# Attended values loaded with the sums, other due times, and queries and keys in a buffer of their own, in a fused attention and mixture-of-experts layer

## The chip, the cores and the metric

One core of a Trainium2 chip. The kernel is one launch. Its time is the device time in microseconds (us) of that core. The core has TensorE (PE; its weight loads are shown apart as PEld), VectorE (DVE), ScalarE (ACT), GpSimd (POOL) and SyncE (SP), each of which works through its own instructions in their order, and 16 DMA engines that the queues of SP, ACT and POOL feed.

## The reference

The input `x` has 4 sequences of 1024 tokens with 256 channels. Two blocks follow each other.

```python
x = x + attn(_layernorm(x), w_attn, w_proj)       # 16 heads of 16, causal, ALiBi bias
x = x + ffn(_layernorm(x), ...)

# ffn, with T, B, C = x.shape: the second attention runs over the 4 sequences, at each token place
qkv = x @ in_proj_w.T + in_proj_b
scores = einsum('tbhd,sbhd->bhts', q, k) * scale   # t, s: the 4 sequences
ctx = einsum('bhts,sbhd->tbhd', softmax(scores), v)
h = _layernorm(x + ctx @ out_w.T + out_b) * ln1_g + ln1_b
probs = softmax(h @ router_w.T + router_b)
assign = max(top_k(probs, 2)[1])                   # one of 8 experts for each token
out = gelu(h @ w1[e].T + b1[e]) @ w2[e].T + b2[e]  # e = assign
return _layernorm(h + out) * ln2_g + ln2_b
```

## The kernel before

Two versions of the layer are in the program: `fast_layer`, which always runs, and `general_layer`, which runs only where a check of the sums asks for it, and did not here. Everything below is `fast_layer`.

**Attention.** The 1024 tokens of a sequence are cut in 4 chunks of 256. A batch is one chunk of one sequence; there are 16, the sequence changing fastest. A unit is what is attended at a time: a whole batch in the first three chunks (units 0 to 11), one block of 128 tokens in the last chunk (units 12 to 19: the first block of the four sequences, then the second). For each unit and each group g of 4 heads, in rounds of 512 columns, `score` makes products of keys and queries (`sk<-slots`), ACT takes the exponential (`p<-sk`), POOL zeroes what is not causal (L1005), and `weigh` makes products with the values (`pv<-p,v`). Keys and queries of the next unit are loaded into the `slots` buffers by SP (L958), as soon as the scores of the current one have been issued; the loads go by way of a copy in DRAM (`k`), which is written from `kq`, a copy that DVE makes of TensorE's projection.

**The end of a unit.** Values carry a column of ones, so each head's sum of exponentials comes out of the same product. The result `yt` is stored to DRAM (`y`, L1057). Then, each at a due time: `load_sums` (L1064) loads the sums, a row per head, from `y`; `invert` (L1071) has DVE take the reciprocal and stores it to DRAM (`r`); `load_y` (L1079) loads the reciprocals, spread over the channels (`su`, L1090), and the attended values, turned (`yc`, L1093); `divide` (L1096) multiplies them on DVE; `project` (L1105) multiplies with `wp` on TensorE and adds to `x` (`x<-x,op`). Unit 19, the last, goes another way: `normalise` makes its sums with a product and inverts them on DVE, `project_slots` projects.

**Fronts.** A front (`front`, L1573) is the second attention and the choice of expert for one block of 128 token places of all four sequences; there are 8 (0 to 7). It is a generator; each `yield` names the kind of the next piece (`E`, `P`: DVE; `D`, `d`: products; `N`: ACT; `R`: a square root on POOL) and its cost. Its pieces: norm statistics; `u` (normalised); `utF`, transposes of `u` to `ut`; the projection into `qkv` (queries, keys, values and router columns together); four scores on DVE (`pr`, `sc`); softmax; four weighted sums on DVE (`pv`, `ctx`); transposes; the output projection `ao`; a norm; the choice (`key` to `hot`); counting and ranks (`place`). The buffer `qkv` exists once: a front may begin the projection (`DQ`) only when `held["qkv"]` is free, which it becomes after the weighted sums (L1720). Front 7 (`last`) puts norms and copies on ACT.

**Experts.** After front 5 a first table of tiles of 128 tokens is made (`tabulate_first`: `count`, `own`, `in_tile`, `who_first`, `rows`, `at_w`), after front 7 a second (`tabulate_rest`: `who`). A tile is gathered by POOL (`given`, L1839), turned (`mtp`), goes through the two weights (`hid`, `oe`), is normed by DVE and scattered to `out` by POOL (L1955). 18 tiles belong to the first table, 20 to the second. The first four tiles load their own weights (L1857); all weights are loaded after attention (L2310). All this lies after attention.

**The order.** The order on each engine is written by a planner in the program while it is built. It keeps an imagined clock of PE, DVE and ACT. In the main loop (L2273) two rounds of scores and one of weighing form a step, with an `E_slot` (L2219) after each scoring, in which due DVE work and transfers are emitted, and one `D_slot` (L2231), in which due products are. `attended` (L2153) puts a unit's end on the lists `due_E` and `due_D` at the times of L76 after it was attended. `take_E` and `take_D` emit pieces of at most two running fronts. A store that is not asked for sooner waits one `E_slot` (`issue_stores`). `projected` (L2164) starts the fronts of a chunk once its fourth sequence is projected. After the main loop what is left of the lists is emitted (L2294), then `normalise(2)` and `(3)`, then the tail's own loop interleaves the last fronts and the tiles.

Of the kernel before, what the change touches and what calls it, by code (L numbers as in the profile page):

```python
# [74 lines left out]
AHEAD, EARLY_BY, ROOT, OF_D = 1.0, 0.2, 1.4, 0.35  # L75
SUMS_BY, INVERTED_BY, Y_BY, DIVIDED_BY, PROJECTED_BY = 7.0, 14.0, 18.0, 29.0, 31.0  # L76

# [528 lines left out]
def fast_layer(ctx: ExitStack, tc: tile.TileContext, odd, x, wq, wk, wv, wp, w_in, w_out, w_r,  # L606
# [127 lines left out]
    nc.gpsimd.iota(number_i, pattern=[[0, 1]], base=0, channel_multiplier=1)  # L734
    pos = fact.tile([P, T], F32, tag="pr", name="pos", bufs=2)
    nc.gpsimd.iota(
# [324 lines left out]
    def heads_of(n):  # L1061
        return y_of[n].rearrange("g p w -> (g p) w").rearrange("(h s) w -> h s w", s=S)

    def load_sums(u):  # L1064
        part_of_row = units[u][2] * H
        issue_stores(("y", u))
        nc.sync.dma_start(
            sums[u], heads_of(u)[:, D].rearrange("h (k w) -> h k w", w=part_of_row)
        )

    def invert(u):  # L1071
# [6 lines left out]

    def load_y(u):  # L1079


        width = units[u][2] * P
        yc, su = (
            ends.tile([P, CC, W], F32, tag=tag, name=f"{tag}_{u}", bufs=2)[:, :, :width]
            for tag in ("yc", "su")
        )
        some = P // D
        for cc in range(CC):
            at = slice(some * cc, some * (cc + 1))
            nc.sync.dma_start(  # L1090
                su[:, cc], r_of[u][at].unsqueeze(1).to_broadcast([some, D, width])
            )
            nc.sync.dma_start(yc[:, cc], heads_of(u)[at, :D])  # L1093
        held["y", u] = yc, su

    def divide(u):  # L1096
        yc, su = held["y", u]
        nc.vector.tensor_tensor(yc, yc, su, ALU.mult)
# [6 lines left out]
    def project(u):  # L1105
        yc, _ = held.pop(("y", u))
        pm = bank(f"op_{u}")
        for i in range(units[u][2]):
            for cc in range(CC):
                nc.tensor.matmul(  # L1110
                    pm[:, i * C:(i + 1) * C], yc[:, cc, i * P:(i + 1) * P], wp_sb[:, cc],
                    start=cc == 0, stop=cc == CC - 1,
                )
        add_attended(u, pm)
# [352 lines left out]
    def prepare_biases(stage):  # L1467
# [24 lines left out]
        n, width = src.shape  # L1492
        rest = fact.tile([n, width], F32, tag="pr", name="rest", bufs=2)
        nc.vector.tensor_copy(rest, src)
# [78 lines left out]
    def front(i, fact, more, last):  # L1573
# [45 lines left out]
        yield "DQ" if more else "D", 2.8  # L1619
        qkv = fact.tile([P, B, 3 * C + E], F32, tag="qkv", name=f"qkv_{i}")  # L1620

        def projected_qkv(t, lo, hi):
            pq = bank(f"qkvp_{i}_{t}")[:, :hi - lo]
            for cc in range(CC):
                nc.tensor.matmul(
                    pq, ut[:, cc, t * P:(t + 1) * P], w_in_sb[:, cc, lo:hi],
                    start=cc == 0, stop=cc == CC - 1,
                )
                if not lo + cc:
                    nc.tensor.matmul(pq[:, :C], ones_bf, in_bf, start=False, stop=False)  # L1630
            if lo and not last:
                nc.vector.tensor_copy(qkv[:, t, lo:hi], pq)
            else:
                nc.scalar.copy(qkv[:, t, lo:hi], pq)

# [7 lines left out]
        def routed():  # L1643
            nc.vector.tensor_tensor(
                u_[:, :, C:], qkv[:, :, 3 * C:], wide(router["b_out"]), ALU.add
            )
# [6 lines left out]
        for t in range(B):  # L1653
            yield "E", 2.4, 0.9 if last else 0.0
            if last:
                projected_qkv(t, QC, 3 * C + E)
            pr = fact.tile([P, B, C], F32, tag="pr", name=f"pr_{i}_{t}", bufs=2)
            nc.vector.tensor_tensor(pr, wide(qkv[:, t, 0:C]), qkv[:, :, C:2 * C], ALU.mult)
            nc.vector.tensor_reduce(
                sc[:, t], pr.rearrange("p s (h d) -> p s h d", d=D), AX.X, ALU.add  # L1660
            )
        yield "E", 1.1
        over_s = lambda a: a.rearrange("p t s h -> p t h s")
# [14 lines left out]
        def weighted(t):  # L1678
            pr = fact.tile([P, B, C], F32, tag="pr", name=f"pv_{i}_{t}", bufs=2)
            nc.vector.tensor_tensor(  # L1680
                pr.rearrange("p s (h d) -> p s h d", d=D),
                qkv[:, :, 2 * C:3 * C].rearrange("p s (h d) -> p s h d", d=D),
                sc[:, t].unsqueeze(3).to_broadcast([P, B, H, D]),
                ALU.mult,
            )
            return pr
# [26 lines left out]
        else:  # L1713
            ctx_ = fact.tile([P, B, C], F32, tag="ctx", name=f"ctx_{i}")
            for t in range(B):
# [3 lines left out]
                nc.vector.tensor_tensor(ctx_[:, t], pr[:, 0], pr[:, 1], ALU.add)  # L1719
        if more:  # L1720
            held.pop(("qkv",))
        if not last:
# [376 lines left out]

    def take_D(cost):  # L2100

        for it in list(running):
            while it.kind[0] in "Dd":
                if it.kind == "DQ" and ("qkv",) in held:
                    break
                if it.kind != "d" and it.ready > time["PE"] + EARLY_BY:
                    break
                if cost and cost + it.cost > D_SLOT:
                    break
                if it.kind == "DQ":  # L2110
                    held["qkv",] = True
                cost += it.cost
                end = product(it.cost, it.next)
                it.ready = max(end + READ, time["DVE"])
            if it.kind == "end":
                running.remove(it)
# [36 lines left out]
    def attended(u, at):  # L2153
        size = units[u][2]
        if u == last_unit:
            return
        for by, what, cost in (
            (SUMS_BY, load_sums, 0.0), (INVERTED_BY, invert, 0.3), (Y_BY, load_y, 0.0),
            (DIVIDED_BY, divide, 0.5),
        ):  # L2160
            due_E.append((at + by, cost, lambda what=what: what(u)))
        due_D.append((at + PROJECTED_BY, 0.9 * size, lambda: projected(u)))

    def projected(u):  # L2164
        n, i, size = units[u]
        c, b = batches[n]
        project(u)
        if b == B - 1:
            queue.extend(front(PC * c + i + k, fact, 1, False) for k in range(size))

# [59 lines left out]

    def D_slot(p):  # L2231
        todo = of_D.pop(p, []) + pop_due(due_D, time["PE"])
        for cost, what in todo:
            product(cost, what)
        take_D(sum(cost for cost, _ in todo))

# [36 lines left out]
    for p in range(len(rounds) // 2):  # L2273
        then = p < len(rounds) // 2 - 1
        score_next(2 * p)
        E_slot(2 * p)
        D_slot(p)
        fill()
# [14 lines left out]
    assert not of_E and not of_D, (sorted(of_E), sorted(of_D))  # L2293
    for _, what in pop_due(due_E + [], 1e9) + pop_due(due_D + [], 1e9):  # L2294
        what()
    for it in running:
        it.ready = 0.0
    for g in range(2, G):
        normalise(g)
    load_sums(last_unit)  # L2300
# [207 lines left out]
```

## Time and profile before

| | us |
|---|---|
| median of 3 runs | 827.63 |
| lowest, highest | 824.45, 828.9 |
| profiled execution | 827.67 |
| its span | 825.9 |
| PE, PEld busy | 708.6, 532.4 |
| DVE, ACT, POOL busy | 544.8, 416.5, 253.6 |
| last product of attention begins (`pv`, after a wait of 2.86) | 617.66 |
| last addition of attention into x (`x<-x,op`) | 632.57 |
| first transposed expert tile (`mtp`) | 667.26 |
| choice of expert of the last front (`hot`) | 723.61 |

The span is the time from the first to the last instruction of the profiled execution; what lies around it makes the difference to its device time. A slice of the page is a fortieth of the span, a digit is a tenth of it busy. In the timeline a line gives the start, the length, the engine, the line, the operation, the output and inputs by the program's names without numbers, the shapes, and in brackets how long the engine had been idle and who ended that. Line 587 is a helper through which nearly all instructions of PE, DVE and ACT are recorded, so they are told apart by their tiles.

### The profile page before, as it was taken

How to read it: one execution, taken by the hardware profiler on the slowest of the kernel's cores; microseconds unless marked ns; L12 is line 12 of the kernel's file. 1: busy time of each engine (PE TensorE's matmuls, PEld its weight loads, DVE VectorE, ACT ScalarE, POOL GpSimd, SP SyncE). 2: the span in 40 equal slices, each digit the busy share in tenths (PEclk: the TensorE clock that was granted, in tenths of full speed). 3: DMA queues.
4: the chain of work that ended last, by engine and by line, in shares of the span. 5: the costliest groups of instructions: out<-in, count | busy, mean ns of one | idle time of the engine just before them, and what ended most of it. 6: DMA issues, size and time to landing. Idle time of an engine off the chain costs nothing. (4 is left out here: it accounts for less than half of the span.)

```text
span 825.9 us, 22497 instructions
## 1 busy us (share of the span) xinstructions
PE 708.6 (86%) x8917; PEld 532.4 (64%) x8917; DVE 544.8 (66%) x1316; ACT 416.5 (50%) x625; POOL 253.6 (31%) x360
## 2 busy tenths in 40 slices
PE   3988878999999999998998998999983689677882
PEld 2766656667666656565787876788662368566771
DVE  7335403739489768847966648497684779885663
ACT  1554535647547656635665757487550236233540
POOL 5533211313021222111222211122120235638885
PEclk9899898999999999999999999999995699988996
DMA  7444444435234234423554556255125512234430
GB/s 218 120 149 147 115 126 139 137 98 169 82 105 136 91 97 127 131 74 98 140 157 118 163 162 158 57 156 166 36 75 198 178 47 89 89 96 127 128 97 25
DMA packets 75220, 99.57 MB, mean 121 GB/s; under 512 B 19496, under 2 KB 58723, under 8 KB 74596
## 3 DMA queue, kind: packets, MB, share of 16 engines
q1 hardware_dynamic: 62272, 67.84, 28.3%
q10 hardware_dynamic: 7972, 16.05, 6.2%
q0 software_dynamic: 4864, 14.16, 5.7%
q8 instruction: 73, 1.20, 0.7%
q14 instruction: 39, 0.32, 0.1%
HBM read 61.55 MB, written 35.12 MB: 117 GB/s over the span
## 5 line engine op out<-in xcount | busy, mean ns | idle before, releaser
L587 ACT ACTIVATE p<-sk 128x1024 f32<-128x1024 f32 (+1 forms) x320 | 287.8, 939 | 160.6 <-PE sk L587 139.4
L1005 POOL TENSOR_SCALAR_AFFINE_SELECT p<-p 128x512 f32<-128x512 f32 (+1 forms) x160 | 105.6, 664 | 396.6 <-ACT p L587 394.6
L587 PE MATMUL sk<-slots 32*128 32x128 f32 (+1 forms) x3456 | 181.1, 328 | 21.5 <-DVE kq L587 8.4
L587 PEld LDWEIGHTS sk<-slots 32*128 32x128 f32 x3456 | 137.2, 187 | 65.0 <-issue 24.8
L587 PE MATMUL pv<-p,v 128*32 128x128 f32 (+1 forms) x3456 | 143.4, 312 | 9.9 <-DVE count L587 2.9
L587 PEld LDWEIGHTS pv<-p,v 128*32 128x32 f32 x3456 | 95.9, 110 | 46.9 <-issue 7.8
L587 PE MATMUL qkvp<-w_in,ut 128*128 128x264 f32 (+1 forms) x228 | 80.3, 488 | 0.0
L587 PEld LDWEIGHTS qkvp<-w_in,ut 128*128 128x128 f32 x228 | 40.8, 193 | 26.9 <-issue 22.4
L587 PE MATMUL oe<-w,ge 128*128 (+1 forms) x152 | 43.4, 410 | 14.4 <-DVE given L587 6.0
L587 PE MATMUL qkp<-xt,wqk 128*128 128x256 f32 x224 | 55.5, 392 | 0.2 <-ACT p L587 0.2
L1839 POOL DMA_INDIRECT given<-rows,rows x38 | 43.5, 1144 | 27.4 <-DVE at_t L587 11.4
L587 DVE COPY qkv<-qkvp 128x264 f32<-128x264 f32 x28 | 12.1, 432 | 54.1 <-PE qkvp L587 54.1
L587 PEld LDWEIGHTS qkp<-xt,wqk 128*128 128x128 f32 x224 | 40.9, 191 | 10.5 <-issue 3.3
L587 PE MATMUL hid<-mt,w 128*128 128x128 f32 x304 | 47.2, 293 | 0.4 <-ACT ge L587 0.4
L587 ACT COPY qkv<-qkvp 128x512 f32<-128x512 f32 (+1 forms) x29 | 16.1, 557 | 59.0 <-PE qkvp L587 47.1
L587 PEld LDWEIGHTS hid<-mt,w 128*128 128x128 f32 x304 | 42.2, 201 | 1.9 <-ACT ge L587 0.9
L1955 POOL DMA_INDIRECT out_dram<-o,out_rows x38 | 38.9, 1024 | 8.7 <-issue 5.9
L587 DVE TENSOR_TENSOR pv<-qkv,sc 128x1024 f32<-128x1024 f32 x32 | 40.2, 1257 | 0.6 <-PE ctp L587 0.6
L587 DVE TENSOR_REDUCE sc<-pr 128x64 f32<-128x1024 f32 x32 | 39.0, 1220 | 1.1
L587 DVE TENSOR_TENSOR pr<-qkv 128x1024 f32<-128x1024 f32 x32 | 39.6, 1238 | 0.0
L587 PEld LDWEIGHTS oe<-w,ge 128*128 128x128 f32 x152 | 27.2, 200 | 19.1 <-DVE given L587 7.4
L587 PE MATMUL vp<-wv,xt 128*128 128x256 f32 x128 | 34.4, 414 | 0.0
(316 smaller groups left out, 1017.9 us busy)
## 6 DMA issues: line engine op xcount, KB each, us to landing
slots<-k SPq DMA_DIRECT2D x128, 80.0 KB
k<-kq SPq DMA_DIRECT2D x32, 256.0 KB
v<-v ACTq DMA_DIRECT2D x4, 1152.0 KB
x<-in_x_dram SPq DMA_DIRECT2D x16, 256.0 KB
y<-yt SPq DMA_DIRECT2D x16, 256.0 KB
rows<-x SPq DMA_DIRECT2D x32, 128.0 KB
slots<-k SPq DMA_DIRECT2D x64, 64.0 KB
rows<-u SPq DMA_DIRECT2D x8, 512.0 KB
```

What stands on the lines that cost most here:

```text
L587: ins = made(*args, **kwargs)
L1005: nc.gpsimd.affine_select(blocks, blocks, pattern=[[0, 2], [0, size], [1, P]], compare_op=ALU.is_ge, fill=0.0, base=0, channel_multiplier=-1,)
L1839: nc.gpsimd.indirect_dma_start(out=self.hx, out_offset=None, in_=t.rows_of, in_offset=bass.IndirectOffsetOnAxis(ap=t.rows_[:, self.j:self. ...
L1955: ins = nc.gpsimd.indirect_dma_start(out=out.rearrange("t n c -> (t n) c"), out_offset=bass.IndirectOffsetOnAxis(ap=t.table.out_rows[:, t. ...
```

## The change

- **Due times.** Each due time becomes a pair: one for ordinary units, a sooner one for units that complete a block (sequence 3 of a chunk or block, and unit 18).
- **Loads.** The attended values `yc` are loaded right behind the sums, by a new `load_attended`; `load_y` becomes `load_inverse` and loads `su` alone.
- **Fronts begin block by block**, once a block is projected in all four sequences (`n_projected`), instead of when the fourth sequence's unit is.
- **Two buffers for one.** Queries and keys (`qk`, the old `qkv` buffer) and values with router columns (`vr`, two buffers) are apart; the former is given back after the four scores. To make room, the `pr` buffer, of which there were two, is one; the last front uses `ctx` for every second weighted sum.
- **DVE pieces between products.** `take_D` calls `take_E` after each product of a front.
- **After the main loop** due transfers and DVE work are emitted first, then `normalise`, then due products.

```diff
-SUMS_BY, INVERTED_BY, Y_BY, DIVIDED_BY, PROJECTED_BY = 7.0, 14.0, 18.0, 29.0, 31.0
+SUMS_BY, INVERTED_BY, Y_BY, DIVIDED_BY, PROJECTED_BY = (
+    (5.0, 3.0), (10.0, 7.0), (12.5, 8.0), (19.0, 13.0), (20.5, 14.5)
+)
...
+    def load_attended(u):
+        yc = ends.tile([P, CC, W], F32, tag="yc", name=f"yc_{u}", bufs=2)
+        held["y", u] = yc[:, :, :units[u][2] * P]
+        for cc in range(CC):
+            at = slice(P // D * cc, P // D * (cc + 1))
+            nc.sync.dma_start(held["y", u][:, cc], heads_of(u)[at, :D])
+
     def load_sums(u):
...
+        if u < last_unit:
+            load_attended(u)
...
-    def load_y(u):
+    def load_inverse(u):
         width = units[u][2] * P
-        yc, su = (
-            ends.tile([P, CC, W], F32, tag=tag, name=f"{tag}_{u}", bufs=2)[:, :, :width]
-            for tag in ("yc", "su")
-        )
+        su = ends.tile([P, CC, W], F32, tag="su", name=f"su_{u}", bufs=2)[:, :, :width]
         some = P // D
         for cc in range(CC):
             at = slice(some * cc, some * (cc + 1))
             nc.sync.dma_start(
                 su[:, cc], r_of[u][at].unsqueeze(1).to_broadcast([some, D, width])
             )
-            nc.sync.dma_start(yc[:, cc], heads_of(u)[at, :D])
-        held["y", u] = yc, su
+        held["inverse", u] = su
...
-        qkv = fact.tile([P, B, 3 * C + E], F32, tag="qkv", name=f"qkv_{i}")
+        qk = fact.tile([P, B, QC], F32, tag="qkv", name=f"qkv_{i}")
+        vr = fact.tile([P, B, C + E], F32, tag="vr", name=f"vr_{i}", bufs=2)
...
-            if lo and not last:
-                nc.vector.tensor_copy(qkv[:, t, lo:hi], pq)
+            if not lo:
+                nc.scalar.copy(qk[:, t], pq)
+            elif last:
+                nc.scalar.copy(vr[:, t], pq)
             else:
-                nc.scalar.copy(qkv[:, t, lo:hi], pq)
+                nc.vector.tensor_copy(vr[:, t], pq)
...
-            pr = fact.tile([P, B, C], F32, tag="pr", name=f"pr_{i}_{t}", bufs=2)
-            nc.vector.tensor_tensor(pr, wide(qkv[:, t, 0:C]), qkv[:, :, C:2 * C], ALU.mult)
+            pr = fact.tile([P, B, C], F32, tag="pr", name=f"pr_{i}_{t}")
+            nc.vector.tensor_tensor(pr, wide(qk[:, t, 0:C]), qk[:, :, C:], ALU.mult)
...
+        if more:
+            held.pop(("qkv",))
         yield "E", 1.1
...
-            pr = fact.tile([P, B, C], F32, tag="pr", name=f"pv_{i}_{t}", bufs=2)
+            pr = fact.tile(
+                [P, B, C], F32, tag="ctx" if last and t % 2 else "pr", name=f"pv_{i}_{t}"
+            )
...
-        if more:
-            held.pop(("qkv",))
         if not last:
...
-    def take_D(cost):
+    def take_D(cost, some):
...
                 it.ready = max(end + READ, time["DVE"])
-            if it.kind == "end":
+                take_E(some)
+            if it.kind == "end" and it in running:
...
+        last = batches[units[u][0]][1] == B - 1 or u == last_unit - 1
         for by, what, cost in (
-            (SUMS_BY, load_sums, 0.0), (INVERTED_BY, invert, 0.3), (Y_BY, load_y, 0.0),
+            (SUMS_BY, load_sums, 0.0), (INVERTED_BY, invert, 0.3), (Y_BY, load_inverse, 0.0),
             (DIVIDED_BY, divide, 0.5),
         ):
-            due_E.append((at + by, cost, lambda what=what: what(u)))
-        due_D.append((at + PROJECTED_BY, 0.9 * size, lambda: projected(u)))
+            due_E.append((at + by[last], cost, lambda what=what: what(u)))
+        due_D.append((at + PROJECTED_BY[last], 0.9 * size, lambda: projected(u)))
+
+    n_projected = [0] * NT
...
         project(u)
-        if b == B - 1:
-            queue.extend(front(PC * c + i + k, fact, 1, False) for k in range(size))
+        for k in range(PC * c + i, PC * c + i + size):
+            n_projected[k] += 1
+            if n_projected[k] == B and k < NT - 1:
+                queue.append(front(k, fact, 1, False))
...
-    for _, what in pop_due(due_E + [], 1e9) + pop_due(due_D + [], 1e9):
+    for _, what in pop_due(due_E + [], 1e9):
+        what()
+    for g in range(2, G):
+        normalise(g)
+    for _, what in pop_due(due_D + [], 1e9):
         what()
     for it in running:
         it.ready = 0.0
-    for g in range(2, G):
-        normalise(g)
     load_sums(last_unit)
```

## The prediction

> **What bounds the kernel now.** First the page: the span, the engines, the slices.
>
> ```profile
> span 825.9 us, 22497 instructions
> ...
> PE 708.6 (86%) x8917; PEld 532.4 (64%) x8917; DVE 544.8 (66%) x1316; ACT 416.5 (50%) x625; POOL 253.6 (31%) x360
> ...
> PE   3988878999999999998998998999983689677882
> ...
> DVE  7335403739489768847966648497684779885663
> ...
> PEclk9899898999999999999999999999995699988996
> ```
>
> One slice is 20.6 us. For the first 30 slices TensorE is busy nearly throughout; at 618 us it drops to 4 and 5 tenths, its granted clock falls with it, and from there VectorE (DVE) carries more. So there are two stages, and I cut the span there: attention to 618 us; a hole to the last addition into x (632.6); the last front and the first experts up to its choice of expert (723.7); the rest.
>
> ```profile
> 400.00:618.00 218.00, 204.39 (x4144) 163.34 (x4143) 153.28 (x330) 137.66 (x186) 47.90 (x75) 1.00 0.47 129
> 618.00:632.60 14.60, 8.73 (x76) 6.69 (x68) 4.08 (x11) 0.27 (x1) 0.00 (x0) 0.53 0.56 191
> 632.60:723.70 91.10, 65.25 (x377) 50.86 (x378) 76.12 (x201) 32.44 (x68) 37.83 (x38) 0.87 0.34 107
> 723.70:825.90 102.20, 71.93 (x505) 62.48 (x504) 63.31 (x196) 34.00 (x75) 69.13 (x99) 0.88 0.30 94
> ```
>
> Columns are the busy us of PE, its weight loads, DVE, ACT and POOL, then the granted clock, the DMA share and GB/s. In attention PE works 204 of 218 us. In the hole nothing is at work but a chain of transfers. In the third stretch DVE is busy 76 of 91 us. The timeline shows the hole:
>
> ```profile
> 617.44 0.16 DVE L587 TENSOR_SCALAR count<-sum 128x8 f32<-128x8 f32 x1
> ...
> 617.66 2.74 PE L587 MATMUL pv<-p,v 128*32 128x128 f32 x64 [2.86 <-DVE count L587]
> ...
> 618.71 0.24 DVE L587 RECIPROCAL inverse<-sums 128x16 f32<-128x16 f32 x1
> ...
> 621.19 0.60 SPq L1090 DMA_DIRECT2D su<-r  x1
> ...
> 625.67 0.43 DVE L587 TENSOR_TENSOR yc<-yc,su 128x256 f32<-128x256 f32 x1 [6.71 <-DMA yc<-y]
> ...
> 626.20 2.05 PE L587 MATMUL op<-wp,yc 128*128 128x256 f32 x4 [5.80 <-DVE yc L587]
> ...
> 632.57 0.42 DVE L587 TENSOR_TENSOR x<-x,op 128x256 f32<-128x256 f32 x1 [1.38 <-PE op L587]
> ```
>
> TensorE's last attention product waits 2.86 us for DVE (`count`), because it takes the bank that DVE has not read yet. Then unit 18's sums are inverted only at 618.7; r, su and yc go through the SP queue, DVE gets yc at 625.67, TensorE projects at 626.2, and the last addition into x is at 632.57. Later:
>
> ```profile
> 655.51 1.07 ACT L587 COPY qkv<-qkvp 128x512 f32<-128x512 f32 x2 [11.81 <-DVE pv L587]
> ...
> 667.26 0.38 PE L587 MATMUL mtp<-ident,given 128*128 128x128 f32 x2
> ```
>
> ACT stood 11.8 us because front 7's queries and keys need the one `qkv` buffer, which front 6 gives back only after its weighted values; the first expert tile starts at 667. The chain that ended last runs through front 7:
>
> ```profile
> 723.61 0.20 DVE hot L587
> 723.86 0.25 PE counts_all L587 x4
> ...
> 731.59 1.01 PE who L587 x32
> ```
>
> The choice (`hot`, 723.61) releases the counts and the second table (`who`); the remaining tiles take what is left, 825.9 - 723.6 = 102.3 us.
>
> **The change, part by part.**
>
> *Order of instructions.* The changed program puts on TensorE before the last attention product the same work as before (projections 0 to 17, fronts 0 to 5, front 6 up to its values), plus the first table's `who_first`: 1.29 us by its row (24 matmuls at 642.87). What moves is when: front 6's projections stand behind round 18/1 instead of 19/0. By the exponentials of the profiled run these are at 564.6 and 583.3 us, so 18.7 us sooner. Hence front 6's scores and softmax, two of its four weighted sums and the whole first table pass from the tail into attention on DVE.
>
> *(a) To the last addition into x.* The bank: now DVE reads the first normalising sum, then does inverse_18, the softmax end and two weighted sums (0.24 + 0.57 + 0.55 + 0.42 + 2 x (1.22 + 0.69 + 0.42) = 6.4 us, plus a reciprocal and a product, 0.95 + 0.29) before it reads the second. TensorE writes the first at 605.7, so the second is read by about 605.7 + 7.7 + 0.95 = 614.4: the product's 2.86 us wait goes, and it ends at 614.8 + 2.74 = 617.5. inverse_18 now stands at about 607, so its chain (618.95 to 625.67 = 6.7 us before; no yc between, 6.1) ends at 613, under attention. Left are the copy of yt (0.27), a sum (0.5), two reciprocals and products (2 x 1.25) and the last two projections, which took 1.38 us from yn to x: 617.5 + 4.7 = 622.2. Gain 10.3 us.
>
> *(b) From there to `hot_7`.* Before, 200 DVE instructions summing to 82.6 us; after, 163 and 67.8 us. The 37 that left are: looking up the first table, 10 (3.2 us); its three in_tile steps (1.5); who_f to at_w, 13 (2.7); front 6's softmax, 5 (2.5); two weighted sums, 6 (4.7). Together 14.7 us; rows overlap by 2% where DVE is dense, so 14.5 us. They are hidden under attention, where DVE was busy 153 of 218 us; if that cover were full, they would cost their 14.5 us there.
>
> *(c) DVE's gaps in that stretch* were 10.8 us (3.0 and 2.4 before ao_6, 2.3 before ao_7, 1.4 before ct_6). The ACT wait of 11.8 us did not stop DVE, which set the pace; with the buffer given back at the scores it goes, but I book nothing for it. New are waits with less to fill them: ct_6 behind ACT's four norm steps (2.07), rstd_h_6 on POOL (1.0 to 1.95). Gaps 7 to 18; I take 10.8, no difference.
>
> *(d) Attention itself.* +1.3 for `who_first`. Due times shrink: from inverse to division 15 us on the plan's clock before, now 9, or 6 for units that complete a block. The exposed chain is 6.1 us, so DVE, and TensorE's projection behind it, can now wait; queued behind DVE's division are the kq copies, for which scores wait, and behind SP's su loads (which wait about 2 us for r to land: 618.99 to 621.19) the next unit's slots. Bounds: none at all, or some waits saved (longest PE gaps now 8.3 us at 119 and 5.9 at 80, both behind DVE's inverse and bias work), -5; to 0.6 us for each of 19 units, +12. I take +2: at units 6 and 11 DVE already waited 4.3 and 5.8 us for yc and TensorE's gaps there stayed under 1.7 us, so most of such a wait is absorbed.
>
> *(e) At nothing:* attended values in the sums' place in the SP queue (38 loads before and after, 0.6 us each; SP waits on PE there anyway); one `pr` buffer for two (written and read by DVE alone, in order; in the last front, where PE reads it, every second goes to the `ctx` buffer); queries/keys and values in two buffers (28 + 29 copies as before).
>
> *(f) Early tiles.* The order puts two tiles' transposes and hid_0_0 ahead of front 6's transposes. Own weights are issued from about 621 (SP first waits for y_19 to land); ctx_6 is ready at 622.2 + 8 = 630. Loads took 650.77 to 666 for all eight; the first must land within 9 us. I book 0; at the worst, all eight before the first, +7.
>
> *(g) After `hot_7`* the orders of PE, DVE and POOL agree, and POOL was not behind (7.7 of 20.6 us busy from 721 to 741): 102.3 us stay.
>
> Sum: 825.9 - 10.3 - 14.5 + 0 + 1.3 + 2 = 804.4 us. The execution took 827.67 with what lies around the span (+1.8); the median of the runs is 827.63. So 806 us.
>
> Beside this: the granted clock was 0.53 in the hole and 0.87 behind it. The Trainium skill (TensorE: Matmul & The Clock Gate, Part 1: The HAM clock gate) says that TensorE drops to half clock after an idle window of some 3.4 us and returns after as long a busy one. By it the shorter hole would also speed the products of front 7 that follow; halving the 2.80 us of its transposes and some 6 us of its projections would make the sum about 802.
>
> Against the change speaks the same skill's DMA: Bandwidth & Descriptors (Issuing engines are not separate DMA queues): transfers of SP and POOL share the same 16 engines. The trace agrees: eight own weights and four gathers (3.68 MB), together from 645 to 670, ran at 147 GB/s in the mean. Here eight own weights, both layers' weights and six gathers now start together; by the page's 436 GB/s their 7.3 MB would take an estimated 17 us, and the sum would be the worst case of (f), 813.
>
> **The rivals.**
>
> *The tail waits for its first weights* (f): for it, PE's order is fixed and front 7 stands behind hid_0_0; against it, the first load is first in the queue. Price +7: 813; with DVE's gaps at 18 instead of 10.8, 820.
>
> *Attention pays it back, slower.* Place: DVE's division and inverse of every unit, with TensorE's projection behind it. For it: DVE waited up to 14.6 us for sums and 4.3 to 6.7 for yc at units 6, 11 and 18, and inverse_16 to division was 7.7 us on the chip where 15 were planned, so 9 may shrink to under 6.1. Against it: at units 6 and 11 TensorE's gap was below 1.7 us. It decides from 22 / 19 = 1.2 us of PE wait for each unit; at 2 us it is 806 + 38 - 2 = 842.
>
> *The moved work does not fit* (DVE was busy 18.7 of 20.6 us from 597 to 618): the last product waits for it, and (a)'s bank gain and (b) are given back: 806 + 2.9 + 14.5 = 823, no change to speak of.
>
> **How the numbers follow.** Forecast (796 to 812) 0.67; weights and gaps (812 to 822) 0.15; no fit (about 823 to 830) 0.05; slower 0.08; below 796 (attention saves 5 and the clock 4) 0.05. A measurement of this kernel can tell 0.5%, 4 us, from no change. Faster 0.87, same 0.04, slower 0.09. Range 795 to 820.
>
> **What would show it.** In the profile after: the last addition into x near 622 to 626; the first transposed tile before 632 instead of 667; slices 31 and 32 of PE well above 4 and 5; `hot` of the last front near 700; still 102 us behind it; ACT's 11.8 us wait gone. Wrong would be: attention's end later than 625, PE gaps over 2 us at projections in many units, or over 18 us of DVE gaps before `hot_7`.

## The result, and the profile after

| | before | after |
|---|---|---|
| median, us | 827.15 (4 runs) | 851.08 (4 runs) |
| lowest, highest | 824.45, 828.9 | 845.14, 853.6 |
| span of the profiled execution | 825.9 | 849.2 |
| last attention product ends | 620.4 | 667.4 |
| last addition of attention into x begins | 632.57 | 672.61 |
| `hot` of the last front | 723.61 | 747.06 |

The change made the kernel slower: ratio 1.028, 95% interval 1.022 to 1.034. The page of the changed kernel:

```profile
span 849.2 us, 22479 instructions
...
PE 727.0 (86%) x8917; PEld 542.9 (64%) x8917; DVE 540.7 (64%) x1316; ACT 415.8 (49%) x625; POOL 253.0 (30%) x360
...
PE   3888698899979896999896999789998699778892
...
DVE  7335325367974843889781637785749679885663
...
PEclk9898789999989997999998899999998989988997
```

TensorE's dip behind attention (slices 31 and 32 of the page before: 3 and 6 tenths, which the prediction's text gives as 4 and 5) is down to a single 6. In its place there are dips inside attention: slices 5, 12, 16, 22 and 26 show 6 or 7 tenths, where before only slice 6 was under 8, and with them the granted clock falls to 7 and 8. The stretches show how much each is worth. First the kernel before, from 25 us to the end of its last attention product (columns as in the prediction: length; busy us of PE, weight loads, DVE, ACT, POOL; granted clock):

```profile
25.00:620.40 595.40, 553.58 (x7979) 406.40 (x7977) 384.71 (x856) 346.26 (x477) 134.65 (x198) 0.98 0.42 121
```

The same stretch of the changed kernel, then from its last addition into x to the last choice, then the rest:

```profile
25.00:667.50 642.50, 575.96 (x8015) 419.33 (x8011) 394.59 (x894) 346.88 (x478) 134.21 (x199) 0.94 0.39 114
672.60:747.10 74.50, 62.54 (x353) 50.11 (x352) 62.57 (x164) 31.82 (x67) 33.11 (x34) 0.93 0.46 154
747.10:849.20 102.10, 75.28 (x505) 64.25 (x504) 63.28 (x196) 33.81 (x75) 69.70 (x100) 0.88 0.31 94
```

The last two are 16.6 us shorter (91.0 before) and as long as before (102.3). The whole loss is in attention: 642.5 instead of 595.4 us for nearly the same products (8015 instead of 7979). Of these 47 us, 25 are idle time of TensorE (642.5 - 576.0 = 66.5, before 595.4 - 553.6 = 41.8), and 22 are busy time: the 36 products more, and products that took longer at a clock of 0.94 instead of 0.98.

What DVE waited for in the changed kernel (us in all, times, longest):

```profile
DVE yc L589 <- DMA su<-r: 72.9, 12, 10.5
...
DVE inverse L589 <- DMA sums<-y: 15.9, 5, 5.9
```

Before, its divisions waited 19.2 us in 5 times. Now 12 of 19 divisions wait, 6.1 us in the mean. What TensorE waited for shows where that reaches it; a unit's projection (products of `wp` and `yc`) stands under `op`, `vp` or `qkp`:

```profile
PE op L589 <- issue: 25.8, 7, 8.3
...
PE vp L589 <- DVE yc L589: 6.7, 1, 6.7
...
PE qkp L589 <- DVE yc L589: 3.8, 1, 3.8
```

These three rows make 36.3 us of idle time right ahead of projections. Before the change it was 5.9 us up to the end of attention. Unit 11 shows how it comes about, first in the changed kernel's timeline:

```profile
453.24 0.35 DVE L589 RECIPROCAL inverse<-sums 128x32 f32<-128x32 f32 x1 [5.93 <-DMA sums<-y]
...
457.85 1.17 PE L589 MATMUL sk<-slots 32*128 32x128 f32 x32
...
460.07 0.37 SPq L1086 DMA_DIRECT2D r<-inverse  x1
462.68 1.23 SPq L1097 DMA_DIRECT2D su<-r  x2
...
466.56 0.69 DVE L589 TENSOR_TENSOR yc<-yc,su 128x512 f32<-128x512 f32 x1 [10.46 <-DMA su<-r]
...
467.36 3.75 PE L589 MATMUL op<-wp,yc 128*128 128x256 f32 x8 [8.34 <-issue]
```

DVE inverts the sums at 453.24. SP issues the store of the inverse at 460.07, behind loads into `slots`, and the loads that spread it at 462.68; DVE can divide at 466.56, 13.3 us after the inverse. TensorE ran out of scores at 459.0 and stands 8.34 us at the projection. The same unit before:

```profile
437.63 1.99 PE L587 MATMUL vp<-wv,xt 128*128 128x256 f32 x8
...
439.46 0.60 PE L587 MATMUL vp<-ident,xn 128*128 128x128 f32 x4
...
440.96 0.69 DVE L587 TENSOR_TENSOR yc<-yc,su 128x512 f32<-128x512 f32 x1 [5.79 <-DMA yc<-y]
...
441.75 1.97 PE L587 MATMUL op<-wp,yc 128*128 128x256 f32 x8 [1.69 <-issue]
```

DVE waited here too, 5.79 us. But TensorE had the value projection and transposes (`vp`) of another batch ahead of the projection, until 440.0, and lost 1.69 us. The division was not sooner ready; the projection was later in TensorE's order.

The end of attention in the changed kernel:

```profile
663.72 3.70 PE L589 MATMUL pv<-p,v 128*32 128x128 f32 x128
...
672.41 0.38 PE L589 MATMUL mtp<-ident,given 128*128 128x128 f32 x2
672.61 0.42 DVE L589 TENSOR_TENSOR x<-x,op 128x256 f32<-128x256 f32 x1 [0.46 <-issue]
```

The last attention product runs without a wait, the last addition follows 5.2 us after its end (12.2 before), the first tile's transpose is issued at once (667.26 before).

### The profile page after: what moved, and what is told of

It is laid out like the page before. It is cut to its first block, busy times and chain, and to the rows that moved or that the text cites. A ratio compares the mean times of both kernels' runs of the same rounds, so it can differ in the third digit from the quotient of the medians.

```text
span 849.2 us, 22479 instructions
## 1 busy us (share of the span) xinstructions
PE 727.0 (86%) x8917; PEld 542.9 (64%) x8917; DVE 540.7 (64%) x1316; ACT 415.8 (49%) x625; POOL 253.0 (30%) x360
## 5 line engine op out<-in xcount | busy, mean ns | idle before, releaser
L1007 POOL TENSOR_SCALAR_AFFINE_SELECT p<-p 128x512 f32<-128x512 f32 (+1 forms) x160 | 103.1, 649 | 473.8 <-ACT p L589 472.3
L589 PE MATMUL sk<-slots 32*128 32x128 f32 (+1 forms) x3456 | 184.1, 332 | 17.9 <-ACT p L589 8.1
L589 PEld LDWEIGHTS sk<-slots 32*128 32x128 f32 x3456 | 139.4, 192 | 64.1 <-issue 26.7
L589 PE MATMUL pv<-p,v 128*32 128x128 f32 (+1 forms) x3456 | 147.0, 318 | 9.9 <-ACT p L589 3.6
L589 PE MATMUL qkvp<-w_in,ut 128*128 128x264 f32 (+1 forms) x224 | 76.8, 481 | 0.0
L589 DVE TENSOR_TENSOR yc<-yc,su 128x512 f32<-128x512 f32 (+1 forms) x19 | 11.2, 591 | 72.9 <-DMA su<-r 72.9
L589 PE MATMUL op<-wp,yc 128*128 128x256 f32 x76 | 26.8, 504 | 25.8 <-issue 25.8
L589 DVE COPY vr<-qkvp 128x264 f32<-128x264 f32 x28 | 12.1, 431 | 49.1 <-PE qkvp L589 49.1
L589 DVE TENSOR_TENSOR pv<-vr,sc 128x1024 f32<-128x1024 f32 x32 | 39.8, 1242 | 0.5 <-PE ctp L589 0.3
L589 ACT COPY qkv<-qkvp 128x512 f32<-128x512 f32 x24 | 14.0, 585 | 50.3 <-PE qkvp L589 49.1
```

Of the source, the lines that this page charges most:

```text
L589: ins = made(*args, **kwargs)
L1007: nc.gpsimd.affine_select(blocks, blocks, pattern=[[0, 2], [0, size], [1, P]], compare_op=ALU.is_ge, fill=0.0, base=0, channel_multiplier=-1,)
```

## The experiments

Fifteen kernels were run. "Waits" are DVE's idle times ended by the last of the transfers that a division needs (us, times); "gaps" TensorE's idle time from its first product to the end of the last attention product; "ends" that end; "choice" the time from the last addition into x to the last `hot`. All but the median and the ratio come from the one profiled execution. Idle time ahead of a division that the profile puts down to something else is left out of "waits"; it is over 1 us in all in kernels 2 (7.3 + 0.4), 6 (7.6), 13 (4.3) and 14 (9.1).

| kernel | median | ratio to before (95%) | waits | gaps | ends | choice |
|---|---|---|---|---|---|---|
| before | 827.15 | 1 | 19.2, 5 | 47.7 | 620.4 | 91.0 |
| the change | 851.08 | 1.022 to 1.034 | 72.9, 12 | 73.9 | 667.4 | 74.5 |
| 1: old due times | 824.57 | 0.992 to 0.999 | 19.0, 4 | 40.7 | 622.6 | 85.5 |
| 2: before, new due times | 857.06 | 1.035 to 1.044 | 69.5, 11 | 77.3 | 667.5 | 80.4 |
| 3: late division | 823.34 | 0.995 to 1.000 | none | 46.0 | 626.6 | 88.5 |
| 4: soon for units 15, 18 | 805.01 | 0.970 to 0.984 | 3.0, 2 | 45.7 | 623.6 | 73.2 |
| 5: late projection | 828.38 | 0.997 to 1.003 | 50.6, 10 | 49.0 | 632.7 | 85.9 |
| 6: same distances, later | 856.98 | 1.033 to 1.042 | 52.3, 9 | 59.4 | 646.8 | 86.2 |
| 7: soon for 3, 7, 11, 15, 18 | 831.56 | 1.000 to 1.006 | 41.6, 7 | 63.0 | 649.1 | 64.4 |
| 8: division in the middle | 804.34 | 0.967 to 0.975 | 6.0, 2 | 42.4 | 622.3 | 74.4 |
| 9: 8, late release | 807.24 | 0.967 to 0.979 | 1.7, 1 | 47.4 | 626.9 | 64.3 |
| 10: 8, old order at the end | 803.42 | 0.966 to 0.975 | 5.3, 1 | 45.1 | 623.5 | 74.3 |
| 11: 8, values behind the inverse | 803.44 | 0.967 to 0.976 | 9.8, 2 | 43.0 | 620.0 | 74.1 |
| 12: 8, no pieces between | 821.36 | 0.989 to 0.995 | 1.5, 2 | 46.4 | 622.3 | 86.6 |
| 13: the change, other queue | 854.29 | 1.029 to 1.036 | 59.5, 10 | 78.2 | 674.0 | 74.4 |
| 14: 8, other queue | 803.48 | 0.967 to 0.978 | 1.4, 1 | 41.6 | 618.9 | 74.4 |
| 15: before, two parts of 8 | 808.27 | 0.973 to 0.979 | 4.2, 2 | 46.6 | 626.4 | 64.4 |

**1 and 2: the due times against everything else.** In both the diff is the line of the due times. The first is the changed kernel with the old ones.

```diff
+SUMS_BY, INVERTED_BY, Y_BY, DIVIDED_BY, PROJECTED_BY = (
+    (7.0, 7.0), (14.0, 14.0), (18.0, 18.0), (29.0, 29.0), (31.0, 31.0)
+)
```

> The changed kernel with the due times of before for every unit (7, 14, 18, 29, 31); everything else of the change stays. Theory T (the short due times make DVE wait at divisions, and TensorE behind it): DVE's wait for su, 72.9 us in 12 waits in the changed kernel, falls below 20; the last attention product ends near 620 instead of 667; time 815 to 832. Rival B (two buffers, fronts block by block and DVE pieces between products spoil attention): the last attention product still ends after 650, time 845 or more. Rival S (loading the attended values with the sums spoils SP's queue): as rival B.

The second is the kernel before with the change's due times and no more.

> The kernel before with nothing but the new due times. Theory T: attention's end comes 30 us or more later than 620, DVE waits over 50 us in all for yc or su, time 845 to 870 (without the buffer split the tail gains nothing but the last chain). Rivals B and S: attention's end within 8 us of before, time 815 to 830.

Measured 824.57 and 857.06, attention's ends at 622.6 and 667.5, waits 19.0 and 69.5. The due times alone make the loss; the buffers, the moved loads and the pieces between products together cost attention 2 us (622.6 against 620.4). Rivals B and S are out.

**3 and 5: which of the due times.** In 3 sums, inverse and loads stay sooner, division and projection go back. In 5 the division stays sooner as well.

```diff
 # 3
+    (5.0, 3.0), (10.0, 7.0), (12.5, 8.0), (29.0, 29.0), (31.0, 31.0)
 # 5
+    (5.0, 3.0), (10.0, 7.0), (12.5, 8.0), (19.0, 13.0), (31.0, 31.0)
```

> The changed kernel with the division and projection back at 29 and 31, but sums, inverse and loads at their new, sooner times. Theory T, in the form that DVE's division in its in-order queue is the place: DVE's waits for su nearly vanish (below 15 us), last attention product ends at 615 to 630, time 812 to 832. A rival within T, that it is the sooner sums and inverse (DVE's inverse waits for the y store, SP's queue stands on it): time stays above 840, with DVE's waits for sums above 30 us.

> The changed kernel with its sooner division (19 and 13) but the projections back at 31. If the loss comes about at TensorE's projection, which stands in TensorE's order right behind a division that DVE is late with, DVE's waits for su stay above 50 us, but TensorE has other products first: time 815 to 832. If the loss comes about through DVE itself (the copies of keys, queries and normalised rows queued behind the waiting division), the time stays at 840 to 858 with TensorE's gaps at scores and transposes.

With 3 no division waits, and the time is 823.34: sooner sums and inverses are harmless. With 5 DVE still waits 50.6 us in ten divisions, but attention ends at 632.7 and the time is 828.38. Unit 11 of kernel 5 in the timeline:

```profile
436.45 0.69 DVE L589 TENSOR_TENSOR yc<-yc,su 128x512 f32<-128x512 f32 x1 [9.61 <-DMA su<-r]
...
438.13 0.94 PE L589 MATMUL sk<-slots 32*128 32x128 f32 x20 [2.27 <-DVE u L589]
...
453.61 1.89 PE L589 MATMUL op<-wp,yc 128*128 128x256 f32 x8
```

DVE waits 9.61 us, nearly as in the change (10.46). TensorE stands 2.27 us, goes through scores, products and projections, and meets unit 11's projection at 453.6, long after the division. So a waiting division alone costs little (632.7 against 626.6 in kernel 3: 6 us for 50.6 us of waits); most of the loss is made at the projection, which stood 1.5 us on the plan's clock behind the division.

**6: sooner, or closer?** All times later, distances as in the change.

```diff
+    (15.0, 19.0), (20.0, 23.0), (22.5, 24.0), (29.0, 29.0), (31.0, 31.0)
```

> The changed kernel with the five due times moved as a whole by 10 (ordinary units: 15, 20, 22.5, 29, 30-31) and 16 (units that complete a block: 19, 23, 24, 29, 31), so that a division is as late as before the change, and as close behind its inverse as after it (9 and 6). If the distance from inverse to division sets the loss: DVE's waits for su above 50 us, time 838 to 858. If only the place of division and projection within the unit does: waits below 20 us, time 815 to 832.

The division is as late as before the change, and DVE waits all the same:

```profile
DVE yc L589 <- DMA su<-r: 52.3, 9, 10.7
```

Time 856.98. So it is the distance from inverse to division, 9 and 6 us on the plan's clock, that makes DVE wait, and not the place in the unit. But the time is made up otherwise than with the change. Attention ends 26 us later than before, with the change 47; but the tail gains less than with the change, because the last units' ends were moved 10 to 16 us later: from the end of attention to the last addition it takes 17 us (5.2 with the change), and the choice 86.2 (74.5). What makes the other 21 us in attention where division and projection are sooner as well was not taken apart.

**4, 7 and 8: how many units, and how close.** 4 and 7 keep the old times for ordinary units and the soon ones, closest of all (6 us from inverse to division), for units that complete a block: in 4 for units 15 and 18 alone, in 7 for all five. 8 has the change's times with divisions at 24 and 19.

```diff
 # 4 and 7
+    (7.0, 3.0), (14.0, 7.0), (18.0, 8.0), (29.0, 13.0), (31.0, 14.5)
 # 4
+        last = last and u >= 15
 # 8
+    (5.0, 3.0), (10.0, 7.0), (12.5, 8.0), (24.0, 19.0), (25.5, 20.5)
```

> The changed kernel with the soon times kept only for units 15 and 18, which complete the last two blocks; all other units at the old times. Theory T: attention loses at most 6 us against before, the tail keeps most of its gain (front 6 begins early), time 805 to 822, below both kernels. Rivals B and S: 840 or more.

> The changed kernel with the soon times for all five units that complete a block (3, 7, 11, 15, 18) and the old times for the other fourteen. At 48 us over 19 units (2.5 us for each), units 3, 7 and 11 add 7.5 us to the 805 of the run with units 15 and 18 alone: 808 to 817. If fronts that begin sooner make up for it, 800 to 808; if the completing units are the bulk of the loss, over 825.

> The changed kernel with divisions at 24 (ordinary) and 19 (completing), projections at 25.5 and 20.5, the sums and inverses left at the sooner times: distance from inverse to division 14 and 12, near the 15 of before. If the distance sets the loss: DVE's waits for su below 20 us, last attention product at 620 to 632, time 800 to 815. If the loss grows evenly with the time that divisions are made sooner (about half of it here): 825 to 840.

Kernel 8 is at 804.34 and kernel 4 at 805.01, both well under the kernel before. A distance of 14 and 12 takes the waits to 6.0 us; the loss goes by the distance, and not evenly with how much sooner a division is. Kernel 7 missed its forecast of 808 to 817: 831.56. Units 3, 7 and 11 waited 12.1, 5.1 and 9.1 us, and the ordinary units right behind two of them, 4 and 12, waited 6.0 and 5.5; attention ended 25 us later than in kernel 4, more for each unit than the 2.5 us that the change's loss gives over all 19. Of the 25 us 17 are gaps of TensorE, above all two at projections, 13.4 us behind unit 3's division and 6.9 us behind unit 7's; the rest are products that took longer. Kernel 8's page and waits:

```profile
PE 712.1 (89%) x8917; PEld 533.4 (66%) x8917; DVE 545.7 (68%) x1316; ACT 415.6 (52%) x625; POOL 257.0 (32%) x360
...
PE   3987879999999999999999899999997798878782
...
PEclk9899989999999999999899999999999799999997
```

```profile
DVE yc L589 <- DMA su<-r: 6.0, 2, 4.9
```

and its unit 11:

```profile
433.71 0.71 DVE L589 TENSOR_TENSOR yc<-yc,su 128x512 f32<-128x512 f32 x1 [4.92 <-DMA su<-r]
...
433.71 1.99 PE L589 MATMUL qkp<-xt,wqk 128*128 128x256 f32 x8
...
435.55 1.89 PE L589 MATMUL qkp<-wp,yc 128*128 128x256 f32 x8
```

It waits here too, 4.92 us, but TensorE has queries and keys of another batch to project in the meantime and takes up the unit's projection at 435.55 without a gap.

**9 to 12: which parts make the gain.** Each undoes one part in kernel 8.

```diff
 # 9: after the four scores
-        if more:
-            held.pop(("qkv",))
 # 9: after the weighted sums
+        if more:
+            held.pop(("qkv",))
 # 10: after the main loop
+    for _, what in pop_due(due_E + [], 1e9) + pop_due(due_D + [], 1e9):
+        what()
+    for it in running:
+        it.ready = 0.0
+    for g in range(2, G):
+        normalise(g)
 # 11: in load_sums, and at the end of load_inverse
-        if u < last_unit:
-            load_attended(u)
+        load_attended(u)
 # 12: in take_D
-                take_E(some)
```

> The version with divisions at 24 and 19 (804), with one part undone: a front gives its queries and keys back only after its weighted values, as before the change; the two buffers stay. If the tail's gain is front 6's work moved into attention and it moves because of the early release (step b of the prediction, 14.5 us): front 6's choice is no longer near 652 us but after 675, the time from the last addition into x to the last choice is 85 us or more instead of 74, time 814 to 824. If the sooner projection alone moves it: 801 to 808.

> The same version with the old order after the main loop (due transfers, due products, then the normalising sums). Step a of the prediction: TensorE's last attention product waits for DVE again behind the projection, and the last addition into x comes 3 to 6 us later: 806 to 811. If this order is worth nothing because the sooner division has already taken unit 18 out of the end: 802 to 806.

> The same version with the attended values loaded behind the spread inverse again (su, su, yc, yc), not with the sums. Step e of the prediction booked the moved loads at nothing: 802 to 807. If the 1.3 us that the two loads add to the chain from inverse to division count at every unit although the distance is 12 to 14 us: 812 to 830.

> The same version without the DVE pieces between the products of a front. The prediction booked nothing for them: 801 to 809. If they are what lets front 6 be done early: 812 or more, with front 6's choice after 665 us.

Kernels 10 and 11 are the same as kernel 8 to within their intervals. So is 9 (807.24): the early release is not needed, against what I expected. Front 6 makes its choice as early, and front 7 sooner (695.4), though what is left behind it then takes 111 us instead of 103. Only the pieces between products matter: without them front 6's choice comes at 695.0 instead of 651.7 us, and the time is 821.36. The `hot` of fronts 6 and 7, in kernel 8 and in kernel 12:

```profile
651.68 0.19 DVE L589 TENSOR_TENSOR hot<-low_con,expert 128x32 bf16<-128x32 f32 x1
...
701.25 0.19 DVE L589 TENSOR_TENSOR hot<-low_con,expert 128x32 bf16<-128x32 f32 x1
```

```profile
694.98 0.19 DVE L589 TENSOR_TENSOR hot<-low_con,expert 128x32 bf16<-128x32 f32 x1
...
713.04 0.19 DVE L589 TENSOR_TENSOR hot<-low_con,expert 128x32 bf16<-128x32 f32 x1
```

Kernels 1 and 3 have the pieces and are at 824 and 823 all the same, with front 6's choice at 695. So both are needed, the pieces and the sooner times. Unit 15, whose projection front 6 waits for, is added into x at 565.3 and 565.6 us there, in kernels 4, 8, 9 and 15 between 546.7 and 559.7; that this is what holds front 6 back was not tested by itself.

**13 and 14: is it SP's queue?** Store and spreading loads of the inverse are issued by POOL.

```diff
-        nc.sync.dma_start(
+        nc.gpsimd.dma_start(
             r_of[u].rearrange("h (k w) -> (h k) w", w=width), inverse[:, :width]
...
-            nc.sync.dma_start(
+            nc.gpsimd.dma_start(
                 su[:, cc], r_of[u][at].unsqueeze(1).to_broadcast([some, D, width])
```

> The changed kernel, due times as in the change, with the store of the inverse (r) and the loads that spread it (su) issued by POOL instead of SP. In the changed kernel the 12 divisions that waited began 9.2 us after their inverse in the mean, although the bare chain is 6 us; r was issued up to 11 us after the inverse, behind loads of keys and queries on SP. If SP's order is the larger part of the late division: DVE's waits for su below 35 us, last attention product before 642 us, time 815 to 835. If the bare chain alone is too long for the distance: waits of 45 us or more, time 838 to 855. If POOL's own work is now late behind the waiting transfers: over 855.

> The version with divisions at 24 and 19 (804) with r and su issued by POOL. With 12 to 14 us from inverse to division DVE waits little, so a shorter chain should give little: 800 to 806. If POOL's masks come late behind the waiting transfers: 808 or more.

Kernel 13, what DVE waited for:

```profile
DVE yc L589 <- DMA su<-r: 59.5, 10, 9.8
```

The waits fell by 13 us, and nothing of the time: 854.29. At unit 11, where SP's order had lengthened the chain, it fell from 13.3 to 10.0 us. But where nothing stood ahead POOL's way is itself longer, 7.2 and 6.5 us at units 7 and 8 (5.9 and 5.4 by SP), and the ten divisions that waited began 8.8 us after their inverse in the mean, hardly less than 9.2. So the other queue does not help; how much SP's order alone costs, this run does not tell. Kernel 14 shows no difference from 8.

**15: the least that makes the gain.** The kernel before, with the due times of kernel 8 and `take_E(some)` between the products, and nothing else of the change.

> The kernel before with only two things: the due times of the 804 version (5/3, 10/7, 12.5/8, 24/19, 25.5/20.5) and the DVE pieces between the products of a front. One qkv buffer given back at the end, two pr buffers, attended values with su, fronts four sequences at a time and the old order after the main loop stay. If these two parts make the whole gain: 798 to 810. If the second buffer and the fronts block by block are needed together: 815 to 826.

808.27: nearly all of the gain. The second buffer, the fronts block by block, the moved loads and the order at the end together are worth 4 us by the medians, and by the ends of the two intervals anything from nothing to 10 us.

## Why the prediction was wrong

Forecast 806, measured 851.08. Step by step:

- **(a) to the last addition into x.** The bank wait went, and from the last product's end to the addition it took 5.2 us where 4.7 were worked out. Right in size, but not by the new order: kernel 1 has the order and the old times and took 12.2 us, as before the change; kernel 2 has the old order and the new times and took 5.2. The sooner due times take unit 18 out of the end.
- **(b) and (c), to the last choice.** 74.5 us where 91.0 - 14.5 = 76.5 were forecast; DVE's instructions there sum to 68.1 us, 67.8 by the forecast. The size was right, the reason only in part: I read ACT's 11.8 us wait for `qkv` and put the move of front 6 down to the early release. Kernel 9 shows, with the due times of kernel 8, that it moves without it, and kernel 12 that it does not move without the DVE pieces between products, for which no cost or gain was worked out.
- **(d) attention.** This is the step that failed: +1.3 and +2 forecast, 47 measured at the end of the last product (with the bank wait of 2.9 us, which went, already taken off). Its bounds ended at +12. Two of its sentences were wrong. "Most of such a wait is absorbed", from units 6 and 11, took the cover to belong to the wait. It belonged to the two projections' place in TensorE's order, behind 2.4 us of `vp` and more, and the change moved the projections as well. And the exposed chain of 6.1 us, measured in the quiet end of the kernel, was taken as the length everywhere: in the twelve divisions that waited, inverse to division took 5.2 to 17.7 us, 9.2 in the mean. Nor did the chip keep the plan's 9 and 6 us. A due time only sets an instruction's place in the order, and DVE takes it up as soon as what stands ahead is done: less its wait, it came to these divisions 0.3 to 8.4 us after the inverse began, 3.1 in the mean. At units 3, 4, 7 and 8 the division is the very next instruction; unit 8:

```profile
320.25 0.35 DVE L589 RECIPROCAL inverse<-sums 128x32 f32<-128x32 f32 x1
325.68 0.69 DVE L589 TENSOR_TENSOR yc<-yc,su 128x512 f32<-128x512 f32 x1 [5.08 <-DMA su<-r]
```

The sign that the prediction had named, gaps of TensorE over 2 us at projections in many units, is there at units 1, 3, 4, 6, 8 and 11: 3.0 to 8.3 us.
- **(e)** held: the moved loads (kernel 11) and the buffers (kernel 1) cost nothing to speak of.
- **(f)** held in part: `mtp` follows the last projections at once, but TensorE then waits for the first tile's weights, as the rival "the tail waits for its first weights" had it, and front 6's transposes stand behind:

```profile
678.10 1.22 PE L589 MATMUL hid<-mt,w 128*128 128x128 f32 x4 [4.28 <-DMA w<-in_w_dram]
```

It was booked at nothing; the stretch to the last choice came out 2 us under the forecast all the same. The rival "does not fit" is not seen: the last product waits for nothing.
- **(g)** 102.3 forecast, 102.1 measured.
- One reading of the page beside this: in the hole before the change not only transfers were at work; by the prediction's own row TensorE is busy 8.73 of its 14.60 us.

So the rival "Attention pays it back, slower" came about, in the place it named. It was priced at 2 us of TensorE's waiting for each of 19 units, 842. The waiting at projections is 36.3 / 19 = 1.9, so that price was near; attention lost 47 / 19 = 2.5 for each, and with this the same sum gives 806 + 47 - 3.3 = 850. Its condition, 9 us shrinking to under the chain, stood in the text with the row for it (7.7 us on the chip where 15 were planned). That ratio, put on 9, gives 4.6 us, less than the chain's 6.1; the forecast should have followed it.

The gain itself was there to be had: with distances of 14 and 12 (kernel 8) the kernel takes 804.34, within 2 us of the forecast for the change itself. That the time comes out there does not make step (d) right, which was about other due times. The fastest medians, 803.4 to 805.0 in kernels 4, 8, 10, 11 and 14, can't be told apart.

## What to carry to other kernels

Before a due time is shortened, compare the distance between the two ends of a chain of transfers, as the chip keeps it and not as the plan has it, with the chain's length on the chip at that place, not at its quietest; a wait in an engine's order is free only as long as the next engine has other work issued ahead of what depends on it. When a row shows a wait that cost nothing, look up what stood ahead of it, and whether the change moves that too. A bundle of edits is worth taking apart even when it loses: here the pieces between products, with moderately sooner times, make nearly all of the gain (kernel 15), and the times of division and projection all of the loss (kernel 3).

## What the hardware showed beside this

A gap on TensorE cost more than its length. The granted clock of the changed kernel around unit 11's gap (459.0 to 467.4), in windows of 1 us:

```profile
461.00:462.00 1.00, 0.00 (x0) 0.00 (x0) 0.00 (x0) 0.05 (x1) 0.00 (x0) 1.00 0.21 21
462.00:463.00 1.00, 0.00 (x0) 0.00 (x0) 0.00 (x0) 0.00 (x0) 0.00 (x0) 0.62 0.00 0
...
471.00:472.00 1.00, 1.00 (x17) 0.96 (x20) 0.85 (x2) 0.00 (x0) 0.00 (x0) 0.50 0.00 0
472.00:473.00 1.00, 1.00 (x32) 0.83 (x28) 0.93 (x5) 0.21 (x1) 0.00 (x0) 0.76 0.06 16
```

The clock is 1.00 until 462 and 0.62 in the window shown, so it was halved at about 462.2, 3.2 us after TensorE fell idle. It is 0.50 until 472 and full again from about 472.5, 5.1 us after the projection began. The projection took 3.75 us where the same eight products took 1.97 before. So the 8.34 us gap cost an estimated 2.6 us more (half of 5.1). Over attention, kernel 1 is the nearest to compare with: it has the same products and differs in the due times alone. From the first product to the end of the last one of attention it has 40.7 us of gaps and 574.0 us of products at a mean clock of 0.97, the changed kernel 73.9 and 585.4 at 0.94. So of the 45 us between them 33 are gaps and 11 are products that took longer.

The Trainium skill (TensorE: Matmul & The Clock Gate, Part 1: The HAM clock gate) has a window of some 3.4 us, which runs freely, for both directions. This trace agrees. Up to the last attention product it has thirteen stretches at half clock; each is 3.41, 6.83 or 10.24 us long, one, two or three times 3.41, and they begin and end on one grid of that step (before the change there are four up to 618 us, 23.9 us in all; here it is 78.5). Unit 11's lasts from 462.24 to 472.48, three steps. In the step ahead of the fall, from 458.83, TensorE worked 0.19 us. Its work began again in the middle of a step (1.71 of the 3.42 us from 465.65), and the clock came back only at the end of the next, which it worked throughout: 5.1 us where one window would be 3.4.

Open: how much of the products' longer time goes back to the slower clock alone; no kernel was run in which TensorE's gaps are there without the fall of the clock.
